# Sending the attention's rows of largest scores and of sums from ScalarE's queue

## The chip, the cores and the metric

The kernel runs on one core of a Trainium2 chip. The core has a matrix engine (TensorE, PE in the profile), a vector engine (VectorE, DVE), an engine for functions of one input (ScalarE, ACT), a general engine (GpSimd, POOL) and SyncE (SP), which in this kernel only issues transfers. Each engine works through its own queue of instructions in order, and waits there for semaphores that other engines or transfers raise. The metric is the device time in microseconds (us); before the change the median of three runs is 5533.94 us.

## The reference

The input is 64 sequences of 128 tokens with 512 features. One layer is applied: a selective state space block, a cross-attention-like block and a small mixture of experts, each on a layer norm of its input and added to it.

```python
x = x + mamba(layernorm(x))       # in_proj, conv, silu, dt, scan over tokens, gate, out_proj
x = x + xattn(layernorm(x), ctx)
x = x + experts(layernorm(x))     # 8 experts of width 16, the two largest of a softmax
```

The change lies in the second block. Here each sequence is read the other way round: the 128 tokens are the features of the attention (8 heads of 16), and the 512 features are its positions.

```python
x = transpose(mask, (0, 2, 1))                       # positions 512, features 128
q, k, v = split(x @ w_in.T + b_in, 3)                # 8 heads of 16
scores = einsum('bqhd,bkhd->bhqk', q, k) / 4
scores = where(|i - j| <= 64, scores, -largest)      # a band
attn = softmax(scores)
o = einsum('bhqk,bkhd->bqhd', attn, v) @ w_out.T + b_out
out = einsum('nit,io->not', relu(o.T) * encodings, w_ct) + b_ct
```

## The kernel before

The sequences are taken in 32 groups of two (b = 0 and 1). A group has 32 steps of the scan: 8 blocks of 128 inner channels, times 4 quarters of the 16 states. A step (`STEP`, lines 199 to 211) multiplies rows on GpSimd (`by_b`, line 435, tile h), takes four exponentials on ScalarE (`decays`, line 447, tile da), runs two scans and two products on VectorE (`scan` and `by_c`, lines 466 and 471, tile hc; in some steps the product is on GpSimd, line 476), and sums on TensorE (`summed`, line 491, tile yp).

Around the steps stand the "strands" of a group, written as generators that yield between pieces: `front` (layer norm, then in_proj at line 553 into tile pin, convolution), `silu`, `step_size` (dt; it ends in a memset on GpSimd at line 697 and then writes dt and dt·u to DRAM, line 702, as tiles dtd and dud, four transfers each), `gates` (tile pg), `out_proj` (tile po), `attend` and `tail` for each of the two sequences, and `experts` (its router's logits are copied at line 953, tile plv). Work of neighbouring groups overlaps: while group g is attended, the front of the next is computed.

The order is written out by hand. `PLAN` and `STEP` give every piece a position, `in_order` sorts all pieces by it and calls them, and the engines' queues follow that order. So an instruction that waits holds everything that stands behind it on the same engine.

Some PSUM buffers are single: pool `ps_b` (tiles pin, pg, pl and others, from `take_b`) has one, so the next of these matrix products starts only when the last result has been copied out. Pool `ps_a` (the scores sk and sq) has two.

In `attend`, the products q·k are made twice. First `largest` computes them with the query positions on the partitions (sq), and VectorE takes the maxima over keys (line 836, tile mx). TensorE turns these (pm), ScalarE negates them (line 849, tile nm: 8 rows, one a head, of 512), and two transfers (line 852) put them into row 16 of each head's block of 32 rows in tile qT. The tile kT has ones in that row, so when `scores` multiplies 32 rows instead of 16 (line 762, tile sk), the largest score is already subtracted. ScalarE takes the exponential (line 868, tile pe) and TensorE multiplies with the values (line 875, tile pa). The values carry a column of ones, so row 16 of each head's block of the result, copied to tile oT at line 882, is the sum of the exponentials. Two transfers (line 886) send these rows to DRAM (sd). `tail` loads them back in another shape (line 897, tile sm), takes the reciprocal on VectorE, writes that to DRAM (line 902), loads it broadcast (line 906), and GpSimd multiplies oT with it.

All transfers are issued by SyncE, 2321 of them, in one queue: among them the weights wi and wo (lines 301 and 307) and the loads of dtr and dur for each block (line 427). In the program as built, the completion of transfers is counted on eight semaphores, DMAHW0 to DMAHW7, given out in turn; an issue may have to wait for the transfer before it on the same one, and an instruction that waits for a transfer waits for its semaphore.

Of the kernel before, what the change touches and what calls it, by code (L numbers as in the profile page):

```python
# [26 lines left out]
HD = 16  # L27
# [201 lines left out]
def decoder_layer_kernel(  # L229
# [25 lines left out]
    nc = tc.nc  # L255
# [14 lines left out]
    def work(shape, tag, bufs, name):  # L270
        return sb.tile(shape, F32, tag=tag, bufs=bufs, name=name)
# [235 lines left out]
    def take_a(name):  # L507
        return ps_a.tile([P, 2, H], F32, tag="a", name=name)
# [208 lines left out]
    xr, body, oT, sums = {}, {}, {}, {}  # L717
# [34 lines left out]
    def scores(left, right, rows, s, i, name):  # L752

        ps = [take_a(f"{name}_{s}_{i}_{rp}") for rp in range(2)]
        for r in range(4):
            nc.tensor.matmul(  # L756
                ps[r // 2][:, r % 2, :PAIR], identb, mask[:, i * EDGE : i * EDGE + PAIR],
                start=True, stop=False,
            )
        for blk, c0, r0, r1 in PAIRS[i]:  # L760
            for r in range(4):
                nc.tensor.matmul(  # L762
                    ps[r // 2][:, r % 2, c0 : c0 + r1 - r0],
                    left[32 * r : 32 * r + rows, s, blk * P : (blk + 1) * P],
                    right[32 * r : 32 * r + rows, s, r0:r1],
                    start=False, stop=(c0 > 0),
                )
        return ps

    def largest(q, k, s, i, name):  # L770

        ps = [take_a(f"{name}_{s}_{i}_{rp}") for rp in range(2)]
        for r in range(4):
            nc.tensor.matmul(  # L774
                ps[r // 2][:, r % 2, : 2 * WIN], identb, maskq[:, i * WIN : (i + 2) * WIN],
                start=True, stop=False, skip_group_check=True,
            )
        for half in range(4):
            q0 = (4 * i + half) * LOCAL
            k0 = first_key(q0)  # L780
            for r in range(4):
                nc.tensor.matmul(  # L782
                    ps[r // 2][
                        q0 % P : q0 % P + LOCAL, r % 2, half // 2 * WIN : (half // 2 + 1) * WIN
                    ],
                    q[32 * r : 32 * r + HD, s, q0 : q0 + LOCAL],
                    k[32 * r : 32 * r + HD, s, k0 : k0 + WIN],
                    start=False, stop=(half == 3), skip_group_check=True,
                )
        return ps  # L790

    def attend(g, b):

        n = f"{g}_{b}"
        far = g == n_groups - 1 and b == 1
        xl = body[g][:, b, :]
        qk, pqk = [], []
        for a in range(2):
            pqk.append(take_a(f"pqk_{n}_{a}"))
            for s in range(2):  # L800
                nc.tensor.matmul(pqk[a][:, s, :], wqk[:, a, s, :], xl, start=True, stop=True)
        for a in range(2):
            yield
            qk.append(
                work([P, 4, TG], "dtr", 2, f"{'qk'[a]}T_{n}").rearrange("p (h a) t -> p h (a t)", h=2)
                if far
                else work([P, 2, H], "qk"[a] + "T", 1, f"{'qk'[a]}T_{n}")
            )
            for s in range(2):
                nc.scalar.activation(  # L810
                    qk[a][:, s, :], pqk[a][:, s, :], AF.Identity,
                    bias=bqk[:, 2 * a + s : 2 * a + s + 1],
                )
        qT, kT = qk
        yield
        pv = take_a(f"pv_{n}")
        for k in range(4):
            nc.tensor.matmul(
                pv[:, 0, k * P : (k + 1) * P], xl[:, k * P : (k + 1) * P], wv,
                start=True, stop=True,  # L820
            )
        yield
        nc.scalar.copy(
            va[:, :, :, 0:HD], pv[:, 0, :].rearrange("p (k h d) -> p k h d", k=4, h=NH)
        )


        mx = work([P, 4, NH], "mx", 2, f"mx_{n}")
        for s in range(2):
            for i in range(2):  # L830
                yield
                ps = largest(qT, kT, s, i, f"sq_{n}")
                for rp in range(2):
                    yield
                    h0 = 4 * s + 2 * rp
                    nc.vector.tensor_reduce(  # L836
                        mx[:, 2 * i : 2 * i + 2, h0 : h0 + 2].rearrange("p k h -> p h k"),
                        ps[rp][:, :, : 2 * WIN].rearrange("p h (k j) -> p h k j", j=WIN),
                        AX.X, ALU.max,
                    )  # L840
        yield
        pm = take_a(f"pm_{n}")
        for k in range(4):
            nc.tensor.matmul(
                pm[:NH, 0, k * P : (k + 1) * P], mx[:, k, :], ident, start=True, stop=True
            )
        yield
        nm = work([NH, H], "nm", 1, f"nm_{n}")
        nc.scalar.activation(nm, pm[:NH, 0, :], AF.Copy, scale=-1.0)
        yield  # L850
        for s in range(2):
            nc.sync.dma_start(out=qT[HD::32, s, :], in_=nm[4 * s : 4 * s + 4, :])


        oT[g, b] = (
            work([P, 4, TG], "dur", 2, f"oT_{n}").rearrange("p (h a) t -> p h (a t)", h=2)
            if far
            else work([P, 2, H], "oT", 1, f"oT_{n}")
        )
        for s in range(2):  # L860
            pr = {}
            for i in range(2):
                yield
                ps = scores(kT, qT, 32, s, i, f"sk_{n}")
                for rp in range(2):
                    yield
                    t = work([P, 2, PAIR], "pe", 4, f"pe_{n}_{s}_{i}_{rp}")
                    nc.scalar.activation(t, ps[rp][:, :, :PAIR], AF.Exp, scale=0.25)  # L868
                    pr[i, rp] = t
            yield  # L870
            po = take_a(f"pa_{n}_{s}")
            for i in range(2):
                for blk, c0, r0, r1 in PAIRS[i]:
                    for r in range(4):
                        nc.tensor.matmul(  # L875
                            po[32 * r : 32 * r + 32, 0, r0:r1],
                            va[:, blk, 4 * s + r, :],
                            pr[i, r // 2][:, r % 2, c0 : c0 + r1 - r0],
                            start=(blk == 0), stop=(blk == 3), skip_group_check=True,
                        )  # L880
            yield
            nc.scalar.copy(oT[g, b][:, s, :], po[:, 0, :])
        yield
        sums[g, b] = dram.tile([2, 4, H], F32, tag="sd", name=f"sd_{n}")
        for s in range(2):
            nc.sync.dma_start(out=sums[g, b][s], in_=oT[g, b][HD::32, s, :])

    def tail(g, b):

# [124 lines left out]
    def strands(g):  # L1014
        yield "fetch", fetch(g)
        yield "front", front(g)
        for q in range(IC // 2):
            yield f"silu{q}", silu(g, q)
        yield "project", project(g)
        yield "rows_b", states(g, selb, brep, "brep")  # L1020
        yield "rows_c", states(g, selc, crep, "crep")
        for half in range(2):
            yield f"dt{half}", step_size(g, half)
        for q in range(IC // 2):
            yield f"gate{q}", gates(g, q)
        yield "out_proj", out_proj(g)
        for b in range(GB):
            yield f"attend{b}", attend(g, b)
            yield f"tail{b}", tail(g, b)
        yield "experts", experts(g)  # L1030
# [94 lines left out]
```

## Time and profile before

| | |
|---|---|
| median of three runs | 5533.94 us (5499.05, 5533.94, 5534.41) |
| profiled execution, whole time | 5504.05 us |
| its span, first to last instruction | 5502.3 us |
| TensorE clock granted, mean | 0.955 |
| busy: PE, DVE, ACT, POOL | 4658.8, 4529.4, 3994.8, 4577.7 us |
| transfers of line 852 and of line 886 | 128 each, 8 KB each |

The profile is of one execution. A busy time is the sum of an engine's instructions; issuing a transfer is not counted as busy. A row of a timeline or of a group of instructions reads: start, duration, engine, line, operation, tile written <- tiles read, shape, count, and in brackets how long the engine was idle before it and what ended that. "SPq" is the queue of SyncE, PEld the loading of weights into TensorE. The chain of work that ended last follows the program back from its last instruction, at each step to what released it. Two groups' periods can be read from recurring instructions: nm of sequence 1 starts at 1700.04 us and, a group later, at 1863.6 us, some 164 us apart.

### The profile page before, as it was taken

How to read it: one execution, taken by the hardware profiler on the slowest of the kernel's cores; microseconds unless marked ns; L12 is line 12 of the kernel's file. 1: busy time of each engine (PE TensorE's matmuls, PEld its weight loads, DVE VectorE, ACT ScalarE, POOL GpSimd, SP SyncE). 2: the span in 40 equal slices, each digit the busy share in tenths (PEclk: the TensorE clock that was granted, in tenths of full speed). 3: DMA queues.
4: the chain of work that ended last, by engine and by line, in shares of the span. 5: the costliest groups of instructions: out<-in, count | busy, mean ns of one | idle time of the engine just before them, and what ended most of it. 6: DMA issues, size and time to landing. Idle time of an engine off the chain costs nothing.

```text
span 5502.3 us, 99193 instructions
## 1 busy us (share of the span) xinstructions
PE 4658.8 (85%) x37444; PEld 2598.0 (47%) x37444; DVE 4529.4 (82%) x6001; ACT 3994.8 (73%) x7906; POOL 4577.7 (83%) x2831
## 2 busy tenths in 40 slices
PE   4688888888888888988888898888898888898876
PEld 3344544444544444544444554444454444554433
DVE  2878888889888888888888888888888888888882
ACT  3667777777777777777777777777777777777753
POOL 4988889888889889888889888988888988888960
PEclk7889999999999999999999999999999999999997
DMA  2333334433433433433433433333333333333320
GB/s 86 122 106 121 123 121 130 130 114 118 129 122 122 139 110 119 133 113 127 134 124 111 129 119 124 130 127 114 128 116 121 129 128 113 123 115 123 123 90 21
DMA packets 282225, 650.53 MB, mean 118 GB/s; under 512 B 48912, under 2 KB 116496, under 8 KB 281744
## 3 DMA queue, kind: packets, MB, share of 16 engines
q1 hardware_dynamic: 281744, 644.18, 35.9%
q8 instruction: 294, 4.82, 0.4%
q14 instruction: 187, 1.53, 0.1%
HBM read 557.04 MB, written 85.98 MB: 117 GB/s over the span
## 4 chain that ended last, share of the span: by engine, by line
PE 51%; DVE 21%; ACT 15%; POOL 8%; issue 4%; DMA 0%; DVEq 0%; SPq 0%; POOLq 0%; ACTq 0%
PE pin L553 9%; DVE da L466 8%; PE po L734 7%; ACT da L447 5%; PE yp L491 4%; DVE mx L836 4%; PE pg L553 4%; PE pa L875 4%; PE sk L762 4%; DVE hc L471 3%; PE sk L756 3%; POOL h L435 3%; DVE hc L466 3%; ACT pe L868 3%; POOL lo L689 2%
## 5 line engine op out<-in xcount | busy, mean ns | idle before, releaser
L435 POOL TENSOR_TENSOR h<-dur,brep 128x1024 f32<-128x1024 f32 x1024 | 2415.2, 2375 | 355.6 <-DVE da L466 344.1
L447 ACT ACTIVATE da<-dtr,acol 128x256 f32<-128x256 f32 x4096 | 1932.1, 476 | 582.0 <-DVE hc L471 383.8
L466 DVE TENSOR_TENSOR_SCAN da<-da,h 128x512 f32<-128x512 f32 x1280 | 1559.1, 1224 | 354.9 <-ACT da L447 309.2
L476 POOL TENSOR_TENSOR hc<-hc,crep 128x1024 f32<-128x1024 f32 x384 | 920.4, 2397 | 299.2 <-DVE hc L466 281.6
L466 DVE TENSOR_TENSOR_SCAN hc<-da,h 128x512 f32<-128x512 f32 x768 | 923.3, 1215 | 108.4 <-ACT da L447 52.2
L471 DVE TENSOR_TENSOR hc<-da,crep 128x512 f32<-128x512 f32 x1280 | 867.8, 682 | 120.7 <-PE yp L491 80.6
L491 PE MATMUL yp<-hc,sely 128*32 128x256 f32 x8192 | 691.3, 397 | 124.3 <-POOL hc L476 87.2
L868 ACT ACTIVATE pe<-sk 128x896 f32<-128x896 f32 x512 | 448.6, 909 | 133.0 <-PE sk L762 129.1
L553 PE MATMUL pin<-xnT,wi 128*128 128x256 f32 x2048 | 493.7, 396 | 41.1 <-ACT dt L679 19.3
L553 PE MATMUL pg<-xnT,wi 128*128 128x256 f32 x2048 | 478.1, 387 | 41.0 <-DVE gt L714 41.0
L836 DVE TENSOR_REDUCE mx<-sq 128x4 f32<-128x768 f32 x512 | 465.8, 942 | 53.4 <-PE sq L782 53.4
L734 PE MATMUL po<-wo,y 128*128 128x512 f32 x1024 | 473.0, 605 | 0.0
L553 PEld LDWEIGHTS pin<-xnT,wi 128*128 128x128 f32 x2048 | 391.0, 196 | 147.6 <-ACT dt L679 33.8
L553 PEld LDWEIGHTS pg<-xnT,wi 128*128 128x128 f32 x2048 | 379.9, 190 | 137.3 <-DVE gt L714 56.4
L491 PEld LDWEIGHTS yp<-hc,sely 128*32 128x32 f32 x8192 | 188.7, 109 | 530.6 <-issue 248.9
L774 PE MATMUL sq<-maskq,identb 128*128 128x384 bf16 x1024 | 243.1, 346 | 198.8 <-DVE mx L836 196.0
L602 DVE SCALAR_TENSOR_TENSOR u<-pin,cw,u 128x254 f32<-128x254 f32 (+2 forms) x768 | 308.1, 470 | 65.3 <-ACT u L594 65.3
L734 PEld LDWEIGHTS po<-wo,y 128*128 128x128 f32 x1024 | 187.4, 190 | 227.5 <-issue 225.9
L756 PE MATMUL sk<-mask,identb 128*128 128x448 bf16 x1024 | 243.9, 354 | 45.6 <-ACT pe L868 44.7
L875 PE MATMUL pa<-pe,va 128*32 128x256 f32 (+1 forms) x4096 | 235.9, 357 | 48.9 <-ACT pe L868 48.9
L762 PE MATMUL sk<-qT,kT 32*128 32x192 f32 (+1 forms) x4096 | 267.5, 375 | 1.4 <-DMA qT<-nm 1.3
L782 PE MATMUL sq<-kT,qT 16*64 16x192 f32 x8192 | 260.2, 367 | 0.0
(158 smaller groups left out, 6820.0 us busy)
## 6 DMA issues: line engine op xcount, KB each, us to landing
wi<-in_w_inproj SPq DMA_DIRECT2D x256, 512.0 KB
dtr<-dtd SPq DMA_DIRECT2D x256, 512.0 KB
dur<-dud SPq DMA_DIRECT2D x256, 512.0 KB
wo<-in_w_outproj SPq DMA_DIRECT2D x128, 512.0 KB
dtd<-dt SPq DMA_DIRECT2D x256, 128.0 KB
dud<-e SPq DMA_DIRECT2D x256, 128.0 KB
rc<-rd SPq DMA_DIRECT2D x256, 128.0 KB
xf<-in_x SPq DMA_DIRECT2D x64, 256.0 KB
```

The costliest lines, as they stand in the source:

```text
L435: nc.gpsimd.tensor_tensor(hs[k], dur[g, ib], brep[g, j // 2][:, j % 2, :].unsqueeze(1).to_broadcast([P, 4, TG]), ALU.mult,)
L447: nc.scalar.activation(das[k, half][:, s, :], dtr[g, ib][:, c, :], AF.Exp, scale=acol[:, col : col + 1])
L466: nc.vector.tensor_tensor_scan(flat(to), flat(d), flat(hs[k][:, own, :]), 0.0, ALU.mult, ALU.add)
L471: nc.vector.tensor_tensor(product(k)[:, 2 * half : 2 * half + 2, :], das.pop((k, half)), c_rows(k, 2), ALU.mult)
L476: nc.gpsimd.tensor_tensor(hcs[k], hcs[k], c_rows(k, 4), ALU.mult)
L491: nc.tensor.matmul(yps[g, ib][32 * c : 32 * c + 32, :], sely, h[:, c, :], start=False, stop=(j == NJ - 1), skip_group_check=True,)
L553: nc.tensor.matmul(ps[:, s * TG : (s + 1) * TG], w[:, s, k, :], flat3(xnT[g][:, k, :, :]), start=(k == 0), stop=(k == HC - 1),)
L734: nc.tensor.matmul(po[:, b, :], y[g, c][:, b * P : (b + 1) * P], w[:, c - c2, :], start=(c == 0), stop=(c == IC - 1),)
L762: nc.tensor.matmul(ps[r // 2][:, r % 2, c0 : c0 + r1 - r0], left[32 * r : 32 * r + rows, s, blk * P : (blk + 1) * P], right[32 * r : 32 * ...
L836: nc.vector.tensor_reduce(mx[:, 2 * i : 2 * i + 2, h0 : h0 + 2].rearrange("p k h -> p h k"), ps[rp][:, :, : 2 * WIN].rearrange("p h (k j) ...
L868: nc.scalar.activation(t, ps[rp][:, :, :PAIR], AF.Exp, scale=0.25)
L875: nc.tensor.matmul(po[32 * r : 32 * r + 32, 0, r0:r1], va[:, blk, 4 * s + r, :], pr[i, r // 2][:, r % 2, c0 : c0 + r1 - r0], start=(blk == ...
```

## The change

For each sequence four issues, in two places of `attend`, name ScalarE instead of SyncE as the engine that issues. Their source, destination and size stay, and so does their place in the order of the pieces.

```diff
         nc.scalar.activation(nm, pm[:NH, 0, :], AF.Copy, scale=-1.0)
         yield
         for s in range(2):
-            nc.sync.dma_start(out=qT[HD::32, s, :], in_=nm[4 * s : 4 * s + 4, :])
+            nc.scalar.dma_start(out=qT[HD::32, s, :], in_=nm[4 * s : 4 * s + 4, :])
...
         yield
         sums[g, b] = dram.tile([2, 4, H], F32, tag="sd", name=f"sd_{n}")
         for s in range(2):
-            nc.sync.dma_start(out=sums[g, b][s], in_=oT[g, b][HD::32, s, :])
+            nc.scalar.dma_start(out=sums[g, b][s], in_=oT[g, b][HD::32, s, :])
```

## The prediction

> **What bounds the kernel now.** I read the page first, its busy shares and the chain of work that ended last.
>
> ```profile
> span 5502.3 us, 99193 instructions
> PE 4658.8 (85%) x37444; PEld 2598.0 (47%) x37444; DVE 4529.4 (82%) x6001; ACT 3994.8 (73%) x7906; POOL 4577.7 (83%) x2831
> ...
> PE 51%; DVE 21%; ACT 15%; POOL 8%; issue 4%; DMA 0%; DVEq 0%; SPq 0%; POOLq 0%; ACTq 0%
> ```
>
> No engine is full, and the chain passes from one to another with only 4% of unexplained time. It is a pipeline in which four in-order queues wait for each other. ScalarE holds 15% of the chain although it is the least busy, so a hold of its queue can move the end. SyncE and the DMAs hold 0%.
>
> Next I asked what SyncE's queue waits for (releaser: total us, times, longest), and who waited for tile qT.
>
> ```profile
> SPq L852 <- ACT xfT L944: 442.1, 30, 17.6
> SPq L852 <- ACT da L447: 367.6, 31, 12.6
> ```
>
> ```profile
>   DMA qT<-nm: 4.7, 5
> ```
>
> SyncE stands some 810 us at line 852, but all engines together lost 4.7 us to the landing of those rows. Taking this wait off SyncE is worth 5 us at most.
>
> The question is therefore what ScalarE meets at the two new places. The changed program, as built, has the same order on PE, DVE and POOL; 256 issues leave SyncE's queue and stand in ScalarE's. Each group of two sequences has four places with two issues each: the score rows of sequence 0 (A) and 1 (C), the sum rows of sequence 0 (B) and 1 (D). The built program also shows what each waits for. Transfers are counted on eight counters, DMAHW0 to DMAHW7, and an issue first waits until the transfer before it on its counter has landed. In a middle group the second issue of A follows on its counter the first of the dt writes (line 702, `dtd<-dt`); the two issues of C follow the second and third dt write of the group's other half. These pairs repeat group after group. In the old order SyncE issued the score rows ahead of those dt writes and never met this.
>
> ScalarE and SyncE around C and then A, in order of time (start, duration, instruction):
>
> ```profile
> 1702.82 0.99 ACT L447 ACTIVATE da<-dtr,acol 128x256 f32<-128x256 f32 x2 [1.25 <-DVE hc L471]
> 1705.37 1.73 ACT L868 ACTIVATE pe<-sk 128x896 f32<-128x896 f32 x2 [1.57 <-PE sk L762]
> ```
>
> ```profile
> 1700.65 1.18 SPq L852 DMA_DIRECT2D qT<-nm  x2
> 1703.31 2.30 SPq L702 DMA_DIRECT2D dtd<-dt  x4
> ```
>
> ```profile
> 1787.95 0.56 ACT L944 COPY xfT<-ptc 128x512 f32<-128x512 f32 x1
> 1789.79 0.27 ACT L953 COPY plv<-pl 128x136 f32<-128x136 f32 x1 [1.28 <-PE pl L948]
> ```
>
> ```profile
> 1788.07 1.19 SPq L852 DMA_DIRECT2D qT<-nm  x2
> 1791.80 2.32 SPq L702 DMA_DIRECT2D dtd<-dt  x4
> ```
>
> ScalarE will reach the issue of C at about 1703.4 and the second of A at about 1788.6. The dt writes are only issued from 1703.31 and 1791.80 on, when POOL has finished dt. ScalarE would stand until they have landed. The chain in order of time tells whether this ends late work:
>
> ```profile
> 1704.37 0.98 PE sk L762 x16
> 1705.35 0.02 issue
> 1705.37 1.73 ACT pe L868 x2
> ...
> 1788.05 0.47 ACT xfT L944
> 1788.52 0.04 issue
> 1788.56 1.19 PE pl L948 x8
> ...
> 1791.48 3.65 PE pin L553 x16
> ```
>
> Both places lie on it with gaps of 0.02 to 0.04 us.
>
> **The change part by part.** Landings are read from the trace's counter increments, as the last one ahead of the next issue on the same counter. In the median the first, second and third dt write land 3.54, 4.64 and 5.94 us after issue, and a pair of score rows 1.84 us after issue. An issue of line 852 takes 0.564 us on SyncE, one of line 886 0.534 us (medians).
>
> *Removed from SyncE:* 128 x 0.564 + 128 x 0.534 = 141 us of issuing and the waits above. By the 0% of SPq in the chain I value it at zero (at most 5 us, by the qT row). Behind the removed sum rows stand `sm<-sd` and the loads of dtr and dur, and they still wait for what they waited for.
>
> *Moved to ScalarE, A.* The first issue has an old transfer on its counter and goes at once. The second waits for the first dt write: 1791.80 + 3.6 = 1795.4, plus 0.56 gives 1796.0. The copy of plv behind it stood at 1789.79: 6.2 us late. Queued behind are plv, the router's exp and tanh, then pe and da. PE waits for plv, because the next in_proj takes the single bank that plv frees (pin moves from 1791.5 to about 1796.3); DVE waits for plv and da; POOL, already idle for 8.2 us there on DVE, waits longer. Everything shifts together. The same subtraction in the 31 groups that have the pattern gives 5.0 to 6.4 us in most, median 6.1; group 30 gives 3.6. Sum 184 us.
>
> *C.* The first issue waits for the second dt write: issued 1703.9, landed 1708.6. The rows land 1.84 later, 1710.4, and PE's sk, at 1704.30 before, starts there. The second issue waits for the third dt write, landed 1710.4, and is done at 1711.0. pe needs both, 1710.4 + 1.04 of sk = 1711.5, against 1705.37: 6.1 us late. Over 30 groups the subtraction gives 3.7 to 6.5, median 5.7, sum 172 us.
>
> *B and D.* The counters are long free. At B two issues of 0.53 stand between two da; half a us of it lies beside the da still running, 0.6 remains, and ScalarE idles 0.9 for DVE soon after. Bounds 0 and 0.6, taken 0.3. At D the second issue waits for the copy of oT as it did on SyncE and is through at 1725.7, where the next e started at 1725.38: 0.3. Together 0.6 x 30 = 18 us. The sums' path stays covered: at B `sm` goes about 5 us later than 1816.56, landing near 1823 ahead of DVE's reciprocal near 1825.2. Without that cover it would be up to 2 us more per group.
>
> *Last two sequences.* Two places where the rows go some 2 us later than now, by ScalarE's order (5437.2 instead of 5433.9 in the last): 4 us.
>
> No row shows ScalarE issuing a DMA. The nearest are SyncE's rows, and I take their 0.56; half or double of it (0.28, 1.12), with half of the 256 issues on the path, would move the sum by -36 or +72 us. A hold that is partly filled by other work lowers the sum: POOL could be 1 us further ahead at A (its first silu product started 1.05 after its input), and nothing is found at C, where POOL itself waited on DVE just before the dt work. A landing slowed by the dud writes of SyncE raises it; sum rows behind such writes took 3.3 us instead of 1.8, which is 1.5 x 30 = 45 us at C.
>
> A rule of the Trainium skill speaks against any such loss. "DMA: Bandwidth & Descriptors", section "Issuing engines are not separate DMA queues", says that transfers started by scalar, sync or gpsimd run on the same DMA engines and that spreading them only saves the little time of starting them. By it the change gives or takes next to nothing: 5504. It does not count what stands in the queue ahead of the issue. The trace has that row (SyncE's 810 us), and its price depends on who stands behind it. On SyncE nobody did; on ScalarE pe and da do. I go by the rows.
>
> **Sum.** 184 + 172 + 18 + 4 = 378 us. The profiled execution took 5504.05 us in all, so 5882. The three runs before lie at two levels, 5499 and twice 5534, and the profile belongs to the lower; counted from the median it would be 5912. I take 5890.
>
> **Rivals.**
> 1. *The holds are half filled.* Engines are idle 15 to 27% of the span, and if the A hold is made up by them, only C and the rest stay: 172 + 22 = 194, so 5700 to 5730. For it: POOL runs 97% full through C, so it does not lose all of the hold. Against it: the chain at A and C has no gaps. Chance 0.14.
> 2. *The counters don't bind*, because POOL or SyncE get the dt writes out earlier. Then A costs nothing (SyncE's 1788.07 is ScalarE's own time), C about 1 us (rows issued 1703.4, landed 1705.2 against 1704.30), B and D 0.6: 1.6 x 30 + 4 = 52, 5556 to 5586. Against it: SyncE is not what holds the dt writes; they go 0.1 us after POOL's last memset of dt. Chance 0.07.
> 3. *Faster.* SyncE's queue, freed at line 852, brings its loads of wi, dtr and dur forward. It would win the 5 us above and, if VectorE's waits for the sums (26 us, tile sm) went too, 31: 5473 to 5503. It decides only if holds at A and C stay under 1 us. Against it: loads wait for buffers that ScalarE and PE free (1440 us of SyncE's waits at line 427 are for da), not for their turn. Chance 0.04.
>
> **How the numbers follow.** Main case 0.75, 5890, with own bounds of 5790 and 5990 from issue price, filling and contention. The range reaches down to the first rival, 5695, and leaves rivals 2 and 3 out. What a measurement of this kernel can tell from no change is about 1%, 5479 to 5589: rival 3 is mostly there or just below it, rival 2 within it. So faster 0.02, within 0.08, slower 0.90.
>
> **What would show it.** Right: ScalarE waits at line 852 for dtd writes, about 6 us twice a group; PE's sk and pin and DVE's da show the same idle time; the period of a group goes from 164 to about 176 us; busy times stay and every share falls; SyncE no longer waits at 852. Wrong: ScalarE's queue passes line 852 within 1.2 us, or waits there 6 us while PE and DVE keep their times. What would break it most is dt writes landing before ScalarE arrives.

## The result and the profile after

The changed kernel takes 6109.58 us (median of four runs, 6095.04 to 6119.49); the kernel before, in four runs beside them, 5521.13 us. The ratio is 1.1075 with a 95% interval of 1.1047 to 1.1104: 588 us slower. The forecast of 5890 had the direction and was 220 us short; 6110 lies 120 us above its range. The profiled execution took 6109.47 us, 605 more than the one of before.

The page of the kernel after: span, busy times, and the chain that ended last by engine.

```profile
span 6107.7 us, 99185 instructions
PE 4871.0 (80%) x37444; PEld 2700.8 (44%) x37444; DVE 4514.2 (74%) x6001; ACT 3994.5 (65%) x7906; POOL 4572.4 (75%) x2831
...
PE 32%; POOL 24%; DVE 17%; ACT 13%; DMA 7%; issue 5%; ACTq 1%; SPq 0%; DVEq 0%; POOLq 0%
```

DVE, ACT and POOL are as busy as before, to within some 15 us; their shares fall because the span grew. PE is different: the same 37444 products keep it busy 212 us longer (4658.8 before), and the mean granted clock fell from 0.955 to 0.901. The chain now has 7% of DMA and 1% of ScalarE's queue, where both had 0%.

What the engines waited for after (engine, line, releaser: total us, times, longest), first all engines, then SyncE's queue:

```profile
ACT pe L868 <- PE sk L762: 486.0, 156, 12.5
DVE hc L466 <- ACT da L447: 354.7, 79, 11.4
PE sk L762 <- DMA qT<-nm: 288.3, 35, 10.1
ACT plv L953 <- DMA dtd<-dt: 188.3, 30, 7.5
```

```profile
SPq L702 <- POOL dt L697: 906.1, 64, 15.3
SPq L897 <- DMA sd<-oT: 584.0, 71, 17.5
```

The two holds of the prediction are the third and fourth line. At A, plv stands 30 times for a dt write, 6.3 us each. At C, sk stands for the rows, and pe behind it (486 us), then VectorE behind da (355). In the kernel before, the same two waits were:

```profile
ACT pe L868 <- PE sk L762: 129.1, 139, 3.7
DVE hc L466 <- ACT da L447: 52.2, 84, 3.4
```

SyncE no longer waits at line 852; the 810 us it stood there have turned into other waits, for POOL's dt (104 us before, 906 now) and for the sum rows (85 before, 584 now). Tile qT, for whose landing the engines lost 4.7 us before, now says:

```profile
  DMA qT<-nm: 592.7, 71
```

The total counts the weight loads of PE besides its products, so it is about twice the 288.3 above.

The kernel after in order of time, at C:

```profile
2240.05 0.99 ACT L447 ACTIVATE da<-dtr,acol 128x256 f32<-128x256 f32 x2 [1.25 <-DVE hc L471]
...
2240.69 2.31 SPq L702 DMA_DIRECT2D dtd<-dt  x4
...
2245.93 2.63 ACTq L852 DMA_DIRECT2D qT<-nm  x2
...
2251.33 1.88 PE L762 MATMUL sk<-qT,kT 32*128 32x192 f32 x16 [9.73 <-DMA qT<-nm]
...
2253.24 1.73 ACT L868 ACTIVATE pe<-sk 128x896 f32<-128x896 f32 x2 [12.21 <-PE sk L762]
2254.21 1.71 PE L756 MATMUL sk<-mask,identb 128*128 128x448 bf16 x4 [1.00 <-ACT pe L868]
...
2255.88 1.22 DVE L466 TENSOR_TENSOR_SCAN hc<-da,h 128x512 f32<-128x512 f32 x1 [11.02 <-ACT da L447]
...
2258.74 3.21 PE L875 MATMUL pa<-pe,va 128*32 128x192 f32 x32 [1.00 <-ACT pe L868]
```

ScalarE has nothing to do from 2241 on and first issues at 2245.93. The prediction had the second dt write landed at 1708.6; shifted by the 537.38 us between the dt writes of the two traces (1703.31 and 2240.69) that is 2245.98. The hold itself was right to a tenth. What follows was not: the rows land 5.3 us after their issue instead of 1.84, and then PE works at about half speed: sk 1.88 us (it was 0.98 to 1.04), the mask products 1.71 (0.93 just before the hold), pa 3.21 (1.76 at full clock, in a run below). VectorE and POOL idle for some 11 and 8 us.

At A:

```profile
1976.67 0.59 ACT L944 COPY xfT<-ptc 128x512 f32<-128x512 f32 x1
1976.73 4.86 ACTq L852 DMA_DIRECT2D qT<-nm  x2
1977.47 2.31 SPq L702 DMA_DIRECT2D dtd<-dt  x4
...
1981.63 0.27 ACT L953 COPY plv<-pl 128x136 f32<-128x136 f32 x1 [4.38 <-DMA dtd<-dt]
```

The first issue goes at once, the second after the first dt write, and plv behind it, as forecast.

The clock shows in the view by stretches (stretch: length, busy us and count of PE, PEld, DVE, ACT, POOL, then granted TensorE clock, DMA share, GB/s). C in the kernel before, then the hold of after, the 10.7 us behind it, and the next 8:

```profile
1704.00:1712.00 8.00, 5.72 (x80) 3.24 (x79) 3.74 (x4) 4.79 (x8) 7.73 (x8) 1.00 0.42 119
```

```profile
2241.30:2251.30 10.00, 0.30 (x2) 0.00 (x0) 2.44 (x3) 0.00 (x0) 7.73 (x7) 0.72 0.38 113
2251.30:2262.00 10.70, 8.66 (x72) 4.62 (x76) 1.22 (x1) 4.29 (x6) 4.66 (x2) 0.50 0.13 45
2262.00:2270.00 8.00, 8.00 (x64) 4.71 (x60) 4.80 (x6) 6.67 (x13) 2.36 (x1) 0.96 0.39 131
```

Within the ten idle microseconds the clock falls (0.72 in their mean), is at half (0.50) for the products that the hold has delayed, and is back in the stretch after. A narrower stretch shows that it is at half before the first of these products starts:

```profile
2246.30:2250.00 3.70, 0.00 (x0) 0.00 (x0) 0.00 (x0) 0.00 (x0) 2.90 (x4) 0.50 0.26 76
```

This is no matter of one group: in the 28 middle groups the first sk behind C always takes 1.88 us, and pa takes 3.2 in 25 of them. The Trainium skill ("TensorE: Matmul & The Clock Gate", "What's actually happening") describes this gate: half clock after an idle window of about 3.4 us, full clock after a sustained busy one of about that length. The trace agrees with the fall. The half clock lasts longer than one such window here: 10.7 us, in which PE works in bursts and is idle for 2. How busy PE must be to end it, no run here shows.

The period of a group, from nm of sequence 1 to the next, is 184 us in the median instead of 163.8. Where does that time arise? The start of each ScalarE instruction in a group, less that of the same instruction in the trace of before (medians over the groups), tells how late ScalarE has become. It becomes late by 10.4 us at pe behind C, 1.2 at the next pe and 1.5 at the copy of oT (both behind slow products), about 1.0 at e behind D, and 6.1 at plv behind A; a few small gains and losses leave 20.1 in all. Over 30 groups, 20.1 x 30 = 603 us, near the 605 between the two profiled executions.

### The profile page after: what moved, and what is told of

It reads as the page before. It is cut to its first block, busy times and chain, and to the rows that moved or that the text cites. A ratio compares the mean times of both kernels' runs of the same rounds, so it can differ in the third digit from the quotient of the medians.

```text
span 6107.7 us, 99185 instructions
## 1 busy us (share of the span) xinstructions
PE 4871.0 (80%) x37444; PEld 2700.8 (44%) x37444; DVE 4514.2 (74%) x6001; ACT 3994.5 (65%) x7906; POOL 4572.4 (75%) x2831
## 4 chain that ended last, share of the span: by engine, by line
PE 32%; POOL 24%; DVE 17%; ACT 13%; DMA 7%; issue 5%; ACTq 1%; SPq 0%; DVEq 0%; POOLq 0%
PE pin L553 9%; POOL h L435 8%; DVE da L466 6%; PE po L734 6%; POOL lo L689 4%; ACT da L447 4%; DVE hc L466 4%; DMA dtd<-dt 4%; PE sk L762 4%; POOL hc L476 3%; DVE hc L471 3%; DMA qT<-nm 3%; PE yp L491 3%; PE pa L875 3%; POOL e L692 3%
## 5 line engine op out<-in xcount | busy, mean ns | idle before, releaser
L553 PE MATMUL pin<-xnT,wi 128*128 128x256 f32 x2048 | 542.2, 424 | 161.3 <-ACT plv L953 108.7
L553 PEld LDWEIGHTS pin<-xnT,wi 128*128 128x128 f32 x2048 | 425.7, 213 | 283.9 <-ACT plv L953 120.4
L762 PE MATMUL sk<-qT,kT 32*128 32x192 f32 (+1 forms) x4096 | 317.4, 432 | 288.3 <-DMA qT<-nm 288.3
L762 PEld LDWEIGHTS sk<-qT,kT 32*128 32x128 f32 x4096 | 205.5, 216 | 404.3 <-DMA qT<-nm 304.4
L875 PE MATMUL pa<-pe,va 128*32 128x256 f32 (+1 forms) x4096 | 273.4, 402 | 49.7 <-ACT pe L868 49.7
L756 PE MATMUL sk<-mask,identb 128*128 128x448 bf16 x1024 | 268.4, 384 | 37.1 <-ACT pe L868 36.3
```

Of the source, the lines that this page charges most:

```text
L553: nc.tensor.matmul(ps[:, s * TG : (s + 1) * TG], w[:, s, k, :], flat3(xnT[g][:, k, :, :]), start=(k == 0), stop=(k == HC - 1),)
L762: nc.tensor.matmul(ps[r // 2][:, r % 2, c0 : c0 + r1 - r0], left[32 * r : 32 * r + rows, s, blk * P : (blk + 1) * P], right[32 * r : 32 * ...
L875: nc.tensor.matmul(po[32 * r : 32 * r + 32, 0, r0:r1], va[:, blk, 4 * s + r, :], pr[i, r // 2][:, r % 2, c0 : c0 + r1 - r0], start=(blk == ...
```

## The experiments

**Which edit, which place.** Theory H, that of the prediction: ScalarE's queue stands at line 852 for earlier dt writes. Theory I: an issue from ScalarE costs some 2.3 us by itself, wherever it is. Each edit alone, then the rows of each sequence alone:

```diff
# rows_only: line 852 only
-            nc.sync.dma_start(out=qT[HD::32, s, :], in_=nm[4 * s : 4 * s + 4, :])
+            nc.scalar.dma_start(out=qT[HD::32, s, :], in_=nm[4 * s : 4 * s + 4, :])
# sums_only: line 886 only
-            nc.sync.dma_start(out=sums[g, b][s], in_=oT[g, b][HD::32, s, :])
+            nc.scalar.dma_start(out=sums[g, b][s], in_=oT[g, b][HD::32, s, :])
# rows_seq0 (b == 0) and rows_seq1 (b == 1), line 852 only
+            (nc.scalar if b == 0 else nc.sync).dma_start(out=qT[HD::32, s, :], in_=nm[4 * s : 4 * s + 4, :])
```

> Only the rows of largest scores (line 852) are issued by ScalarE, the sums by SyncE as before. Theory H (ScalarE stands at line 852 until earlier dt writes have landed): nearly the whole loss, 6040 to 6110. Theory I (each issue from ScalarE costs about the same, 588 us over 256 issues, 2.3 us each): half of the loss, about 5815.

> Only the sum rows (line 886) are issued by ScalarE. Theory H: their counters are free when ScalarE arrives, so only the issue itself counts, 0 to 1.2 us a group: 5520 to 5560. Theory I: about 5815.

> Only the score rows of sequence 0 (place A) are issued by ScalarE. Theory H: one hold of about 6 us a group, 31 of them: 5700 to 5730. If the loss of both places comes only together (one hold pushing the other): under 5650.

> Only the score rows of sequence 1 (place C) are issued by ScalarE. Theory H with the late landing and the slower matrix engine seen in the trace (10.4 + 1.2 + 1.5 us a group): 30 x 13 = 390, about 5910. With the predicted 5.7 us alone: about 5690.

The kernel before took 5509.94 us beside them (11 runs, 5499.6 to 5519.7). The score rows alone take 6106.53 (one run), practically the whole loss. The sum rows alone take 5537.8 (8 runs; ratio 1.0049, 1.0033 to 1.0066), 28 us. The rows of sequence 0 take 5711.27 (one run), 201 more: A, put at 184. Those of sequence 1 take 5922.15 (one run), 412 more: C, put at 172. (Singly the parts make 641 us, together 588; they overlap a little.) So the error of the forecast lies mainly in C. Waits of rows_seq0, then of rows_seq1:

```profile
ACT plv L953 <- DMA dtd<-dt: 198.5, 30, 7.5
```

```profile
ACT pe L868 <- PE sk L762: 488.1, 165, 12.5
...
PE sk L762 <- DMA qT<-nm: 281.8, 33, 10.1
```

Each has the wait of its own place at the size of the full change. As many issues move at the sums as at the rows, and cost 28 us against some 600: theory I is out.

**Is it the counter, or the place?** The next pair leaves the rows in place and puts the last pieces of `step_size` later in the written order, so that other transfers precede the rows on their counters; once with the rows and sums on ScalarE, once on SyncE. `early` instead puts the score rows directly behind nm.

```diff
# late_after (with the change), late_before (without): PLAN "dt0", "dt1"
-        -11.87, -11.86, -11.85, -11.382, -11.372, -9.923, -7.354,
+        -11.87, -11.86, -11.85, -11.382, -11.372, -7.4, -6.9,
...
-        1.93, 3.985, 6.026, 6.116, 8.486,
+        1.93, 3.985, 6.026, 8.0, 8.486,
# early (with the change): the piece of line 852, PLAN "attend0" and "attend1", parts of two lines
-        ... 36.526, 36.536, 37.042, 37.052, 37.267,
+        ... 36.526, 36.536, 36.537, 37.052, 37.267,
...
-        ... 52.84, 53.571, 53.581, 53.647,
+        ... 52.84, 52.841, 53.581, 53.647,
```

> All 256 issues on ScalarE, as in the changed kernel, but the last piece of the dt work (the memset on GpSimd and the dt and dt*u writes) is put some 10 us later in the hand-written order, so that in the built program the score rows no longer follow a dt write on their counter but loads that landed long before. Theory H: the holds go and with them most of the loss; left are 256 issues of 0.53 us: 5530 to 5640. Theory I: no change from 6110.

> The same later place of the dt writes, with SyncE issuing all. It is the control for the run with ScalarE: the difference of the two is what the 256 issues cost without holds. Theory H: 5510 to 5570 here, and 0 to 80 less than its partner. Theory I: partner 590 above it.

> The changed kernel with the score rows put directly behind nm in ScalarE's order. In the built program this frees the counter at A (a weight load stands ahead of it) but not at C, where the first two dt writes stand ahead. Theory H: A costs the two issues and the wait for nm, about 1.5 us instead of 6.5, and C stays: 5940 to 5980. Theory I, or a loss that follows from the place in the order: 6110 or more.

late_after takes 5799.29 (1.0547, 1.0524 to 1.0569), late_before 5697.33 (1.0361, 1.0343 to 1.0378), the kernel before 5496.78 beside them. The later dt writes cost 3.6% themselves, so both times lie above what was expected of them. What counts is the difference: with the counters free, the same 256 issues on ScalarE cost 1.0547 - 1.0361 = 0.0186, some 102 us, instead of 588. That is more than the 80 allowed for it, too, but about five sixths of the loss are gone: they are the hold and what follows from it. At A in late_after:

```profile
2236.66 1.10 ACTq L852 DMA_DIRECT2D qT<-nm  x2
2238.38 0.28 ACT L953 COPY plv<-pl 128x136 f32<-128x136 f32 x1 [1.28 <-PE pl L948]
```

Both issues pass in 1.10 us, two times 0.55, close to SyncE's 0.564, and plv waits for its own producer as before the change. The 102 us that are left arise mostly at C: by the same subtraction from the trace of before, ScalarE is 2.5 us late at the first pe behind C and 1.2 more at the second, which over 30 groups is as much as is left. late_before has no such delay there.

`early` takes 5944.51 (one run): A comes out free, because another transfer now precedes it on the counter, and C still holds, now ahead of da, 9.8 us in each of 30 groups:

```profile
ACT da L447 <- DMA dtd<-dt: 295.1, 30, 11.0
```

None of these beats the kernel before.

**Why C costs more than twice its estimate: the clock.** Products of mask and identity, whose result is overwritten, keep PE busy during the hold of C: 38 of them, then 51.

```diff
# warm, warm51 (with the change): in `scores`, before the first products
+        if s == 0 and i == 0 and name.endswith("_1"):
+            for _ in range(38):          # 51 in warm51
+                nc.tensor.matmul(ps[0][:, 0, :PAIR], identb, mask[:, :PAIR], start=True, stop=True)
```

> The changed kernel with 38 more products of the mask with the identity (bf16, 448 columns) on TensorE just ahead of the first scores of sequence 1; they are overwritten by the product that follows, so the result stays. They fill the hold at C. If TensorE runs slow after the hold because it idled, sk takes about 1.04 us again instead of 1.88 and the run gains 2.0 to 2.7 us a group, 60 to 80: about 6040. If the slowness comes from elsewhere, or the filling costs more than it gives: 6110 or more.

> As the kernel with 38 filling products, but 51, so that they last through the hold at C (38 took 7.4 us and left TensorE idle for 2.4 us, after which the granted clock still fell to 0.56 for some 10 us). If idleness of TensorE causes the slow stretch, the clock stays at 1.00 behind the hold, and sk, sk and pa take 1.04, 1.04 and 1.76 us again: 2.5 us a group, 75 us less than the changed kernel, about 6030. If the fall comes from the hold of the other engines or the like, the stretch stays at 0.5 and the time near 6090.

With 38, next to nothing was gained: 6081.13 (1.1064, 1.1047 to 1.108), 28 us by the medians and 6 by the ratios, whose intervals overlap. That lies between the two times expected. Its stretches, the hold and what follows:

```profile
2228.00:2238.20 10.20, 7.81 (x42) 3.82 (x39) 2.73 (x4) 0.06 (x1) 8.10 (x7) 1.00 0.38 111
2238.20:2249.00 10.80, 8.74 (x77) 4.22 (x78) 1.22 (x1) 5.16 (x8) 4.67 (x2) 0.56 0.12 44
```

The filling ends 2.4 us early. The first sk runs at full speed (1.04 us), and then the clock falls all the same: two idle times of 2.4 and 1.0 us, with 1.0 us of work between them, were enough. (In about half of the groups it is back up for pa.) warm51 fills 9.8 us, and with the four mask products behind the filling no gap is left; its stretches, and the products behind the hold (lines are five higher):

```profile
2205.00:2215.00 10.00, 10.00 (x54) 5.00 (x52) 2.56 (x3) 0.00 (x0) 7.62 (x7) 1.00 0.39 116
2215.00:2225.60 10.60, 8.33 (x103) 5.19 (x103) 2.92 (x3) 7.45 (x12) 4.69 (x2) 1.00 0.12 43
```

```profile
2215.03 1.04 PE L767 MATMUL sk<-qT,kT 32*128 32x192 f32 x16
...
2218.34 1.04 PE L767 MATMUL sk<-qT,kT 32*128 32x256 f32 x16
...
2220.39 1.76 PE L880 MATMUL pa<-pe,va 128*32 128x192 f32 x32 [1.00 <-ACT pe L873]
```

The clock stays at 1.00, and the time is 6031.89 (1.0954, 1.0928 to 1.098): 78 us less than after by the medians, 67 by the ratios. That part of the loss is PE's own idleness coming back as half speed. Behind C itself, ScalarE is 9.7 us late at the copy of oT instead of 13.1, which is 102 us over 30 groups; some of it is lost again behind A.

**Why C costs more than twice its estimate: the landing.** The rows of C land 5.3 us after issue. Ahead of them SyncE had issued four dt writes, a weight load (wi) and two dt·u writes, and had begun on a third. Three kernels change what is ahead, each in one run.

```diff
# spread_dud: dt·u writes cut by quarters of the 128 partitions (spread_dt: the dt writes, nm == "du")
-                nc.sync.dma_start(out=d[c].rearrange("i g t -> g i t"), in_=src[:, c, :])
+                if nm == "dt":
+                    nc.sync.dma_start(out=d[c].rearrange("i g t -> g i t"), in_=src[:, c, :])
+                    continue
+                nc.sync.dma_start(
+                    out=d[:, :, c, :].rearrange("c i t -> i c t"), in_=src[32 * c : 32 * c + 32]
+                )
# wi_late: PLAN of the front, the piece of line 301 goes behind the dt·u writes
-        ... -39.387, -39.377, -39.358, ...
+        ... -39.387, -39.377, -39.3, ...
```

> The changed kernel with the four dt*u writes cut by quarters of the partitions instead of by channel blocks, so that each has 32 rows as its outer dimension instead of 4 and more of the 16 DMA engines can share it; the dt writes stay. In the built program the two dt writes stay ahead of the score rows at C on their counters, while at A a weight load stands there now. If the late landing at C (5.3 us) comes from sharing few DMA engines with the dt*u writes: landing 2 to 3.5 us and about 5850 to 5890. If it comes from the dt writes themselves or from the weight load: landing stays near 5.3 and about 5930 to 5950.

> The changed kernel with the weight load that stands between the dt and the dt*u writes (line 301, 512 KB) put behind the dt*u writes in SyncE's order. The dt writes stay ahead of the score rows on their counters. In the changed kernel the rows of C land 5.26 us after issue, 0.1 us from the landing of that load. If that load holds the rows: they land 2 to 4.5 us after issue, with the last dt write at the latest, and the time is 6030 to 6085. If they wait for whatever was issued ahead of them on the same DMA engines, now the first dt*u writes: landing 5 us or more, and 6100 or more.

> The changed kernel with the four dt writes, not the dt*u writes, cut by quarters of the partitions, 32 rows as outer dimension instead of 4. In the built program dt writes stay ahead of both score rows of C on their counters; at A old loads stand there. Theory H: A is free, and the hold at C follows the dt writes: if they land 2 to 3 us after issue instead of 4.6 and 5.9, it shrinks by 2 to 3 us; 5760 to 5880. If the hold at C had another cause than these writes, C stays and the time is near 5940.

spread_dud takes 5930.79 (5502.95 before, beside it). It differs from `after` by A, which came out free as in `early`; its C lands as late as ever (5.6 us), and it takes what `early` takes, to 14 us. The form of the dt·u writes is not the cause. wi_late takes 6095.06, between the two ranges expected and no clear gain; its trace decides. The rows land 5.2 us after issue, now 1.1 behind the first dt·u write (4.1), while the weight load lands at 10.8 (medians). So it is not the load either; with the load out of the way the rows come in behind the next transfer.

spread_dt takes 5839.02, the kernel before 5529.91 beside it. The outermost dimension of a dt write is 4 before the edit and 32 after it. The stretches while dt writes alone are moving, in after and then here, show what that does to the share of the 16 DMA engines that is busy (the last figure but one):

```profile
2242.00:2243.00 1.00, 0.00 (x0) 0.00 (x0) 0.01 (x1) 0.00 (x0) 1.00 (x2) 1.00 0.25 60
```

```profile
2152.00:2153.00 1.00, 0.00 (x0) 0.00 (x0) 0.24 (x1) 0.00 (x0) 1.00 (x1) 1.00 0.92 187
```

The work of four engines is spread over nearly all sixteen. The dt writes land 2.1 to 2.6 us after issue at C instead of 3.6 to 7.3, and ScalarE is let go sooner:

```profile
2160.11 1.73 ACT L873 ACTIVATE pe<-sk 128x896 f32<-128x896 f32 x2 [8.71 <-PE sk L767]
```

pe waits 8.7 us instead of 12.2 and is 7.4 late instead of 10.4; the rows land in 4.5. Against spread_dud, where A is free as well, that is 92 us (by the ratios to the kernels before beside them, 120). A shorter dt write shortens the hold, as theory H has it, and it takes only part of the landing away.

What is it that waits: the rows, or only the report that they have landed? The Trainium skill ("DMA: Bandwidth & Descriptors", "Queues, rings and completion order") says that the counter's increment is written in strong order, behind every earlier write of that DMA engine, whichever queue it came from. That rule alone would hold back the report and not the data. The trace of after shows otherwise. ScalarE's transfers have a queue of their own, q10, which the kernel before does not have. The queues' packets in the 4.07 us behind the issue of 2245.93, then in the next 1.3 us (packets, MB, share of the engines' time):

```profile
q1 hardware_dynamic: 267, 0.38, 30.5%
```

```profile
q1 hardware_dynamic: 85, 0.11, 23.5%
q10 hardware_dynamic: 8, 0.01, 1.8%
```

These eight are the first issue's four rows of 2 KB and four packets of 4 bytes, taken here for the increments. In the median of the groups the first row's packet starts 4.2 us after issue (1.2 in the kernel before), and the small packets follow the rows by 0.1 to 0.3. So the rows themselves are late, and the strong order is not what holds them. Nor do they wait for everything issued before them: they land after 5.3 us, the weight load after 5.1, but the first dt·u write, issued 2.2 us before them, after 6.6. Meanwhile the work of about four DMA engines goes on without a break (0.26 in the stretch from 2246.30 above). Whether the rows' packets stand in line at these engines or are made late on their way there, no run here shows, so that cause stays open.

## Why the prediction was right and wrong

**What SyncE loses is worth nothing:** right. Its 810 us turned into other waits.

**A, 184 us:** right; 201 alone, 188.3 us of waits in the full change, through the second issue and plv. The clock falls there too, which the prediction did not count (PE is busy for 4739.8 us in rows_seq0, 81 more than before), yet the place costs only 17 us above its term.

**B and D, 18 us:** 28 (18 to 36 by its interval), about the upper end of the bounds. D's e comes 1.0 us late instead of 0.3.

**C, 172 us:** the step that failed; 412 alone. Its first sentences hold, the issue comes when forecast. Two terms do not.
- "The rows land 1.84 later, 1710.4": 5.3 us. The 1.84 is the median of rows that SyncE issued ahead of the dt writes. Held back by those very writes, the rows come behind what is moving by then, and their packets start 4.2 us after issue instead of 1.2. The prediction named this, as a 1.5 us risk taken from the sum rows; it is 3.5 x 30 = 105 us.
- "plus 1.04 of sk" and everything behind it: durations of the old profile, at full clock. The sum made PE idle for ten microseconds in every group and nothing in it asked what that does to PE. It is 3.5 us of longer products in a group, 105 us again; keeping the clock up gave back 102 behind C and 67 to 78 of the whole time.

In sum: C costs 412 us against 172 and the 4 of the last two sequences, 236 too many. Landing and clock are 105 each of that; some 26 were not traced further. With 17 at A and 10 at the sums it makes 263, and as the parts measured singly overlap by 53 (641 against 588), 210 remain, from 378 to 588.

**What would show it:** the holds, their places, the idle engines and SyncE's row came as written. "Busy times stay" is wrong for PE (+212 us), and the period is 184 instead of 176, for the same two reasons.

**Rivals.** Half-filled holds: out, A alone costs all of it. Counters that don't bind: out; and its price of 52 us was low, the pair with free counters shows about 102, most of it at C, where ScalarE issues the rows later than SyncE did and they land in 3.4 us. Faster: out.

**The rule that speaks against a loss.** That spreading issues over engines only saves the time of starting them agrees with the landing at C, where ScalarE's rows come behind SyncE's transfers, and says nothing of what this change costs: the issue took its wait with it, and the wait, with what followed from it, cost about 490 of 588 us.

## What to carry to other kernels

Before an issue moves to another engine's queue, list what it waits for there, its counter's earlier transfer included, and who stands behind it; a wait that cost nothing on an idle queue costs its full length on one that the chain passes through. Price a delayed transfer by what is in flight at its new time, not by its landing at the old one. And when a sum makes PE idle for several microseconds, price the products behind the gap at the clock that the gap leaves.

## What the runs showed of the hardware

- An issue of these 8 KB transfers takes about 0.53 us on ScalarE at line 852 and 0.51 at line 886 (0.56 and 0.53 on SyncE): the estimate from SyncE's rows held.
- Writes of 128 KB with an outermost dimension of 4 kept 0.25 of the DMA engines' time busy and landed 3.6 to 7.3 us after issue at C; the same bytes with 32 there kept 0.92 busy and landed in 2.1 to 2.6.
- A small transfer's landing is no constant: 1.8 us ahead of other writes, 5.3 behind them, and then its own packets start 4.2 us after issue.
- Filling three quarters of a PE gap saved little: with 2.4 us left the clock still fell, to 0.56; with none left it stayed at 1.00.
